# A four-part attention stack on one core: cross-attention's mask as its keys' last row, and two batches' rows normalised on ScalarE

## The chip, the core and the metric

The kernel runs on one core of a Trainium2 chip. The metric is the device time of one execution in microseconds; lower is better. Each kernel is executed several times and the median is compared. One execution is also recorded by the hardware profiler; the profile shows, for each engine of the core (TensorE as PE, its weight loads as PEld, VectorE as DVE, ScalarE as ACT, GpSimd as POOL, SyncE as SP, which issues most DMAs), what ran when.

## The reference

The reference chains four attention modules over activations of 8 batches x 256 rows x 128 columns, with a context of 8 x 64 rows x 64 columns. Modules 0 and 1 (a gated memory attention with a layer norm, and a single-head attention) run first, module 3 (an attention normalised over queries, with a layer norm) runs last. Nearly all the time goes to module 2: six layers, each of which is

```
tn = _ln(t, norm_g, norm_b)
t  = _mha(tn, tn, skv, sq, sow, sob, tgt_mask) + t      # self-attention, 16 heads of 64
tn = _ln(t, norm_g, norm_b)
t  = _mha(src, tn, ckv, cq, cow, cob, src_mask) + t     # cross-attention to the 64 context rows
tn = _ln(t, pg, pb)
t  = t + (relu(tn @ w1 + b1) @ w2 + b2)                 # feed-forward, 512 wide
```

where `_ln(x, g, b) = (x - mean) / sqrt(var + 1e-5) * g + b`, and `_mha` replaces scores at mask == 0 by -1e9 ahead of the softmax. The same norm_g and norm_b serve self-attention and cross-attention of all layers. All inputs are float32, the masks int32.

## The kernel before

**An order written out by hand.** The kernel is a plan. `at(tick, phase, fn)` files a step under a tick and a phase within it; at the end all steps are run sorted by tick and phase, and each engine is bound to execute its instructions in exactly that order. A tick is roughly one step of the attention pipeline. Nothing reorders the engines afterwards: an instruction that waits holds up everything behind it on its engine. Buffers are rotating pools: a new tile of a tag takes the place of the oldest, and waits for that one's last reader. PSUM is one pool of four tiles of two banks, for everything TensorE writes.

**A layer.** A layer takes 48 ticks: self-attention 32 (four per batch, `plan_sa`), then cross-attention 16 (two per batch, `plan_ca`), with the feed-forward (`plan_ff`) and the next layer's first self-attention projections laid over cross-attention's ticks. In the text, c is the first of the cross-attention ticks (`T_ca` in the code).

**Self-attention's ticks.** Each has two steps of scores (L939, 16 matmuls each), a VectorE pass that adds the mask and takes row minima of the negated scores (L953, eight instructions, each with a short read of its accumulator), eight exps on ScalarE (L958, each with an accumulator read), two reciprocals on VectorE (L966), eight normalising multiplications on GpSimd (L968), and 32x32 block transposes on VectorE (L978). Values (L994), the copies of the results (L299, L301), the output projection (L1012), its addition (L1019) and the next batch's projections (L902, L921) are spread over the ticks.

**Cross-attention's ticks.** The weights of queries and keys are multiplied together ahead of time, for all heads, and so are those of values and outputs. `plan_ca_weights` does that at the end of self-attention: both packed weights are transposed in blocks (L1057), written to DRAM and fetched back (L1060, L1068), regrouped by GpSimd (L1074) and multiplied on TensorE (`folded`, L1083), which gives AT (tick c-4, copied by ScalarE at L1095) and WVO (tick c-3, copied at L1093). For two batches at a time `keys_both` multiplies AT with the context (L1120, copies at L1126, into tiles of tag q); `make_values` does the same with WVO (L318, L324). Then, in each tick, `plan_weights_64` computes for 128 rows x 16 heads x 64 keys: scores (L356, 16 matmuls of 128x32 weights and 256 columns in four groups of four that run side by side), and behind each group four bfloat16 matmuls that add the mask (L363: weights that are one in the first row and zero below, times a tile `nm2` whose first row holds 0 or -1e30). ScalarE copies the scores to SBUF (L372), VectorE takes the maximum (L374), GpSimd subtracts it (L375), ScalarE takes exp (L381). One tick later VectorE sums (L385) and inverts (L386), GpSimd multiplies (L387); then VectorE transposes in blocks (L395), and a tick after that TensorE multiplies with the values (L429) and VectorE adds the result to the activations (L1145).

**Rows are normalised ahead of use.** `ahead` is called for every batch of every sublayer: mean and variance (L849, L850, L852) on VectorE, the power -0.5 (L859) on GpSimd, the normalised rows `xn` (`normal`), and the transposition on TensorE (L882) with norm_g and norm_b applied as scale and bias per partition by ScalarE (L884). `normal` is done either by ScalarE (L868, which also needs a negated mean, L855, and its product with the power, L862) or by VectorE (L873). Cross-attention and feed-forward use ScalarE, self-attention VectorE.

## Time and profile before

| | |
|---|---|
| median of 3 runs (lowest to highest) | 2411.13 us (2407.03 to 2411.5) |
| the profiled execution's own time | 2410.29 us |
| its span, first to last instruction | 2408.5 us |
| mean granted TensorE clock | 0.987 |
| TensorE busy | 2325.2 us (97%) |
| VectorE busy | 1872.3 us (78%) |
| ScalarE busy | 1707.7 us (71%) |
| GpSimd busy | 1359.1 us (56%) |
| DMA share of the instruction-issued queue q1 | 10.1% of 16 engines' span |

The six layers are nearly equal: the first scores of cross-attention (L356) of the six stand at 396.7, 765.8, 1135.0, 1502.9, 1872.2 and 2240.2 us. Matmuls overlap on TensorE and their ends are modelled, so busy time of PE is not time at its peak, and the busy time of a group of matmuls is not what it adds to the span. What an edit is worth is better read from the chain that ended last: from the last instruction back, at each step to what released it or to the instruction ahead of it on its engine. A group's line reads: line, engine, operation, written tile <- read tiles, shapes, count, busy us and mean ns of one, and the idle time ahead of it with what ended it.

### The profile page before, as it was taken

The numbers are of one execution on the slowest core, as the hardware profiler recorded it, in microseconds if no ns is written. First come the engines' busy times: TensorE is split into PE (matmuls) and PEld (weight loads), VectorE is DVE, ScalarE is ACT, GpSimd is POOL, SyncE is SP. The second block draws the span as 40 slices with busy tenths as digits, with TensorE's granted clock in tenths as the row PEclk, the third lists the DMA queues.
The fourth block names the chain that finished last, engine by engine and source line by source line (L and its number), as shares of the span: only waits on it lengthen the run. The fifth ranks groups of instructions, "written<-read, shape, count | busy, mean of one in ns | idle before, by whom it ended". The sixth has DMA issues, their size and how long they took to land.

```text
span 2408.5 us, 100346 instructions
## 1 busy us (share of the span) xinstructions
PE 2325.2 (97%) x42564; PEld 1719.9 (71%) x42564; DVE 1872.3 (78%) x6237; ACT 1707.7 (71%) x4514; POOL 1359.1 (56%) x2231
## 2 busy tenths in 40 slices
PE   7889999999999999999999999999999999999997
PEld 4557777777777777777777777777777777777775
DVE  5677887777888767888767888767888767888775
ACT  4567777667777667778667778667778667777663
POOL 2444556754556754555764555755555765455665
PEclk9989999999999999999999999999999999999998
DMA  6000022001022001012000012000013000001000
GB/s 180 2 2 20 21 73 65 2 3 30 21 64 66 11 3 30 21 56 73 12 2 26 21 45 87 12 2 18 25 40 89 21 2 18 25 26 42 2 4 16
DMA packets 102834, 76.90 MB, mean 32 GB/s; under 512 B 8113, under 2 KB 96881, under 8 KB 102386
## 3 DMA queue, kind: packets, MB, share of 16 engines
q1 hardware_dynamic: 101794, 70.16, 10.1%
q8 instruction: 335, 5.49, 0.9%
q14 instruction: 113, 0.93, 0.1%
q10 hardware_dynamic: 592, 0.33, 0.1%
HBM read 62.07 MB, written 8.39 MB: 29 GB/s over the span
## 4 chain that ended last, share of the span: by engine, by line
PE 75%; DVE 13%; ACT 5%; POOL 4%; issue 2%; DMA 0%; SPq 0%; POOLq 0%; ACTq 0%; DVEq 0%
PE sc L939 12%; PE mm L902 12%; PE mm L994 12%; PE mm L1012 6%; PE mm L921 6%; PE mm L429 6%; PE sc L356 5%; DVE e L953 3%; PE mm L1178 3%; PE mm L1161 3%; DVE eTc L978 2%; DVE m L374 2%; POOL e L968 2%; PE mm L1120 2%; PE mm L318 2%
## 5 line engine op out<-in xcount | busy, mean ns | idle before, releaser
L968 POOL TENSOR_SCALAR e<-e,rs 128x256 f32<-128x256 f32 x1536 | 702.8, 478 | 706.3 <-DVE rs L966 696.5
L958 ACT ACTIVATE e<-e,mn 128x256 f32<-128x256 f32 x1536 | 758.6, 495 | 151.3 <-DVE mn L953 146.5
L953 DVE CUSTOM_DVE_ANT_0 e<-sc,nm 128x256 f32<-128x256 f32 x1536 | 543.1, 419 | 93.4 <-PE sc L939 92.3
L978 DVE STREAM_TRANSPOSE eTc<-e 128x512 f32<-128x512 f32 x768 | 516.2, 694 | 59.4 <-POOL e L968 58.2
L939 PE MATMUL sc<-k,q 64*32 64x256 f32 x12288 | 380.8, 383 | 2.3 <-DVE o L299 1.3
L994 PE MATMUL mm<-eTc,v 32*64 32x256 f32 x12288 | 363.4, 378 | 5.7 <-ACT AT L1095 3.3
L375 POOL TENSOR_TENSOR e<-e,m 128x1024 f32<-128x1024 f32 x112 | 213.0, 1902 | 262.1 <-DVE m L374 262.1
L994 PEld LDWEIGHTS mm<-eTc,v 32*64 32x64 f32 x12288 | 277.1, 131 | 88.5 <-issue 22.2
L939 PEld LDWEIGHTS sc<-k,q 64*32 64x32 f32 x12288 | 221.8, 107 | 125.3 <-issue 51.4
L374 DVE TENSOR_REDUCE m<-e 128x16 f32<-128x1024 f32 x112 | 136.3, 1217 | 197.0 <-ACT e L372 197.0
L958 ACT ACTIVATION_READ_ACCUMULATOR e<-e,mn 128x1 f32 x1536 | 287.9, 187 | 0.0
L356 PE MATMUL sc<-q,tT 128*32 128x256 f32 x3072 | 217.0, 382 | 3.8 <-DVE t L1019 3.2
L429 PE MATMUL mm<-v,o 128*128 128x128 f32 x1536 | 197.5, 283 | 1.9 <-DVE t L1145 1.7
L429 PEld LDWEIGHTS mm<-v,o 128*128 128x128 f32 x1536 | 183.1, 195 | 19.0 <-issue 9.1
L902 PE MATMUL mm<-tT,w_sk 128*128 128x256 f32 x768 | 189.2, 389 | 0.2 <-PE mm L994 0.2
L1012 PEld LDWEIGHTS mm<-w_sow,o 128*128 128x128 f32 x1536 | 175.1, 192 | 17.6 <-issue 12.3
L921 PE MATMUL mm<-w_sv,tT 128*32 128x256 f32 x3072 | 185.6, 382 | 0.0
L1012 PE MATMUL mm<-w_sow,o 128*128 128x128 f32 x1536 | 183.6, 278 | 1.3 <-ACT WVO L1093 1.3
L387 POOL TENSOR_TENSOR e<-e,r 128x1024 f32<-128x1024 f32 x96 | 182.6, 1902 | 0.5 <-DVE r L386 0.5
L301 ACT COPY v<-mm 128x1024 f32<-128x1024 f32 x96 | 97.1, 1012 | 115.4 <-PE mm L921 115.4
L902 PE MATMUL mm<-tT,w_sq 128*128 128x256 f32 x768 | 173.6, 379 | 0.0
L902 PEld LDWEIGHTS mm<-tT,w_sk 128*128 128x128 f32 x768 | 138.3, 190 | 44.2 <-issue 29.2
(222 smaller groups left out, 3489.4 us busy)
## 6 DMA issues: line engine op xcount, KB each, us to landing
nm<-mask_d SPq DMA_DIRECT2D x192, 128.0 KB
wd<-o SPq DMA_DIRECT2D x48, 128.0 KB
w_sk<-in_L_sa_kv_dram SPq DMA_DIRECT2D x6, 512.0 KB
w_sv<-in_L_sa_kv_dram SPq DMA_DIRECT2D x24, 128.0 KB
w_sq<-in_L_sa_q_dram SPq DMA_DIRECT2D x6, 512.0 KB
w_sow<-in_L_sa_ow_dram SPq DMA_DIRECT2D x6, 512.0 KB
w_ckv<-in_L_ca_kv_dram SPq DMA_DIRECT2D x12, 256.0 KB
w_cq<-in_L_ca_q_dram SPq DMA_DIRECT2D x6, 512.0 KB
```

The costliest lines, as they stand in the source:

```text
L356: nc.tensor.matmul(sc[32 * a : 32 * a + 32, q, :], lhsT=qT()[:, qb * 32 : (qb + 1) * 32], rhs=keys()[:, a].rearrange("p h k -> p (h k)"), ...
L375: nc.gpsimd.tensor_tensor(e, e, m.unsqueeze(2).to_broadcast([P, 16, M]), ALU.subtract)
L429: nc.tensor.matmul(ps[:, :D], lhsT=eT[:, s].rearrange("p q x -> p (q x)"), rhs=vw[:, r, k, g, :], start=(s == 0), stop=(s == 7),)
L902: nc.tensor.matmul(ps[:, i * S : (i + 1) * S], lhsT=w[:, c * P : (c + 1) * P], rhs=st["tT"], start=True, stop=True,)
L921: nc.tensor.matmul(ps[32 * a : 32 * a + 32, i, :], lhsT=st["tT"][:, kb * 32 : (kb + 1) * 32], rhs=sv[:, a].rearrange("p g x -> p (g x)"), ...
L939: nc.tensor.matmul(sc[32 * a : 32 * a + 32, r, j, :], lhsT=st["q"][g][rows, a, qb * 32 : (qb + 1) * 32], rhs=st["k"][g][rows, a, :], start ...
L953: nc.vector.tensor_tensor_reduce(e[:, i, :], sc4[:, i, :], st["nm"][:, 2 * jj + i % 2, :], -1.0, 3.0 * BIG, ALU.add, ALU.min, mn[:, i : i ...
L958: nc.scalar.activation(e[:, i, :], e[:, i, :], AF.Exp, scale=-1.0, bias=mn[:, i : i + 1], accum_out=rs[:, i : i + 1],)
L968: nc.gpsimd.tensor_scalar(e[:, i, :], e[:, i, :], rs[:, i : i + 1], 1.0, ALU.mult, ALU.mult)
L978: nc.vector.transpose(eT[:, r, :, 2 * jj : 2 * jj + 2, :], e[:, 2 * r : 2 * r + 2, :].rearrange("p j (k x) -> p k j x", x=32),)
L994: nc.tensor.matmul(ops[a // 2][r * HD : (r + 1) * HD, a % 2, :S], lhsT=st["v"][kb // 4][rows, kb % 4, (2 * g + r) * HD : (2 * g + r + 1) * ...
L1012: nc.tensor.matmul(st["ps"][:, j * D : (j + 1) * D], lhsT=st["oT"][c // 4][:, c % 4, j * P : (j + 1) * P], rhs=sow[:, c, :], start=(c == 0 ...
```

## The change

**The mask.** The bfloat16 mask matmuls are gone. Instead the mask is added to the keys' last row, and that row meets a constant one on the other side. Normalised rows sum to zero over their 128 columns, so the last column is the negative sum of the others and can be left out if each of the other 127 rows of AT has the last row subtracted. For cross-attention `ahead` therefore gets `last_off` as scale (one, but zero in the last partition) and `last_on` as bias (zero, but one in the last partition) in place of norm_g and norm_b, which go into AT instead: AT is multiplied by norm_g, its last column (over the free dimension, which becomes the keys' last row) is subtracted from all, and the row sum of AT times norm_b is put into the last column. `mask_keys` then adds 0 or -1e30 to the last partition of each batch's keys, with one VectorE operation on partitions 96 to 127. `nm2` is now float32 on all 128 partitions.

**The fold.** The whole of `plan_ca_weights` starts one tick earlier; AT is made at c-5, WVO stays at c-3. The new work on AT lies between: two multiplications, a subtraction and two small copies on GpSimd, a row sum on VectorE. norm_g and norm_b are loaded once more, broadcast over partitions.

**The rows.** Self-attention's rows of batches 0 and 1 are normalised by ScalarE, the others by VectorE as before.

The core of the diff:

```diff
+    norm_rows = const.tile([P, 2, D], F32, tag="norm_rows", name="norm_rows")
+    for i, name in enumerate(("L2_norm_g", "L2_norm_b")):
+        nc.sync.dma_start(out=norm_rows[:, i, :], in_=io[name].partition_broadcast(P))
...
-    nm2 = const.tile([P, B, M], BF16, tag="nm2", name="nm2")
-    nc.vector.memset(nm2, 0.0)
-    ones0 = const.tile([P, 32], BF16, tag="ones0", name="ones0")
...
+    nm2 = const.tile([P, B, M], F32, tag="nm2", name="nm2")
+    last_on = ident[:, P - 1 : P]
+    last_off = const.tile([P, 1], F32, tag="last_off", name="last_off")
+    nc.vector.tensor_scalar(last_off, last_on, -1.0, 1.0, ALU.mult, ALU.add)
+    last_big = const.tile([P, 1], F32, tag="last_big", name="last_big")
+    nc.vector.tensor_scalar(last_big, last_on, -BIG, None, ALU.mult)
...
-                        start=True, stop=False,
-                    )
-                for a in range(4):
-                    nc.tensor.matmul(
-                        sc[32 * a : 32 * a + 32, q, :], lhsT=ones0, rhs=mask,
-                        start=False, stop=True,
+                        start=True, stop=True,
                     )
...
-        nc.vector.tensor_scalar(nm2[0:1], mi, 0.0, -BIG, ALU.is_equal, ALU.mult)
+        nc.vector.tensor_scalar(nm2, mi, 0.0, last_big, ALU.is_equal, ALU.mult)
...
-        ahead(b, (T - 6, 8.3), (T - 5, 2.6), (T - 5, 7.2), norm_g, norm_b, st, False)
+        ahead(b, (T - 6, 8.3), (T - 5, 2.6), (T - 5, 7.2), norm_g, norm_b, st, b < 2)
...
         at(T + 2, 3.6, folded("AT", 0, lambda c: st[1][:, :, c, :], HD ** -0.5))
-        at(T + 3, 3.6, folded("WVO", 1, lambda c: W["ca", l][2][:, c, :]))
+        def rows(i):
+            return norm_rows[:, i].unsqueeze(1).to_broadcast([P, HC, D])
+        def meet_bias():
+            st["z"] = big("q", shape=(P, HC, D))
+            nc.gpsimd.tensor_tensor(st["z"], st["AT"], rows(1), ALU.mult)
+        def sum_bias():
+            st["add"] = sm([P, HC], "add")
+            nc.vector.tensor_reduce(st["add"], st.pop("z"), AX.X, ALU.add)
+        def scale():
+            nc.gpsimd.tensor_tensor(st["AT"], st["AT"], rows(0), ALU.mult)
+        def lose_last():
+            last = sm([P, HC], "last")
+            nc.gpsimd.tensor_copy(last, st["AT"][:, :, D - 1])
+            nc.gpsimd.tensor_tensor(
+                st["AT"], st["AT"], last.unsqueeze(2).to_broadcast([P, HC, D]), ALU.subtract
+            )
+        def put_bias():
+            nc.gpsimd.tensor_copy(st["AT"][:, :, D - 1], st.pop("add"))
+        at(T + 2, 8.05, meet_bias)
+        at(T + 3, 2.35, scale)
+        at(T + 3, 8.05, lose_last)
+        at(T + 3, 8.7, sum_bias)
+        at(T + 4, -0.1, put_bias)
+        at(T + 4, 3.6, folded("WVO", 1, lambda c: W["ca", l][2][:, c, :]))
...
+        def mask_keys():
+            last = keys_of[b][96:].rearrange("p a c k -> p (a c) k")
+            nc.vector.tensor_tensor(
+                last, last, nm2[96:, b].unsqueeze(1).to_broadcast([32, 16, M]), ALU.add
+            )
...
-        ahead(b, (T - 4, 6), (T - 3, 2.95), (T - 2, 2.9), norm_g, norm_b, st)
+        ahead(b, (T - 4, 6), (T - 3, 2.95), (T - 2, 2.9), last_off, last_on, st)
...
+        at(T - 1, 1.9, mask_keys)
...
-        plan_ca_weights(l, T_ca - 6)
+        plan_ca_weights(l, T_ca - 7)
```

More of the change, by code (lines that the diff above doesn't have):

```diff
@@ L262, in load_mask @@
         return nm
-    nm2 = const.tile([P, B, M], BF16, tag="nm2", name="nm2")
-    nc.vector.memset(nm2, 0.0)
-    ones0 = const.tile([P, 32], BF16, tag="ones0", name="ones0")
-    nc.vector.memset(ones0, 0.0)
-    nc.vector.memset(ones0[0:1], 1.0)
+    nm2 = const.tile([P, B, M], F32, tag="nm2", name="nm2")
[4 more added lines that the diff above has]
+    nc.vector.tensor_scalar(last_big, last_on, -BIG, None, ALU.mult)
     def stats(xin, eps):
@@ L327, in values_of, with plan_weights_64 @@
         return vw
-    def plan_weights_64(tick, qt, qT, keys, values, mask, take):
+    def plan_weights_64(tick, qt, qT, keys, values, halves, take):
         tl = {}
@@ L336, in scores @@
             sc = two_banks("sc").rearrange("p (q x) -> p q x", q=4)
-            if mask is None:
+            if halves:
                 for i in range(4):
@@ L392, in turn @@
             e = tl.pop("e").rearrange("p (q h) (k x) -> p (h k) q x", q=4, x=32)
-            eT = big("k" if mask is None else "o", shape=(P, 8, 4, 32))
+            eT = big("k" if halves else "o", shape=(P, 8, 4, 32))
             for i in range(2):
@@ L436, in plan_weights_64 @@
         at(tick, 2, lower)
-        if mask is None:
+        if halves:
             at(tick + 1, 2.05, exps)
@@ L637, in mask_keys @@
         mi = big("q", dtype=I32)
-        mi = mi[0:1, : B * M].rearrange("p (b m) -> p b m", b=B)
-        nc.sync.dma_start(out=mi, in_=io["mask_Bx1xS2_if1"].rearrange("b o m -> o b m"))
-        nc.vector.tensor_scalar(nm2[0:1], mi, 0.0, -BIG, ALU.is_equal, ALU.mult)
+        mi = mi[:, : B * M].rearrange("p (b m) -> p b m", b=B)
+        nc.sync.dma_start(
+            out=mi, in_=io["mask_Bx1xS2_if1"].rearrange("b o m -> (b o) m").partition_broadcast(P)
+        )
+        nc.vector.tensor_scalar(nm2, mi, 0.0, last_big, ALU.is_equal, ALU.mult)
     mask_bf = []
@@ L773, in plan_l0 @@
             plan_weights_64(
-                T + qt, qt, lambda: st["q"], lambda: st["k"], lambda: st["VW"], None,
+                T + qt, qt, lambda: st["q"], lambda: st["k"], lambda: st["VW"], True,
                 lambda ps, qt=qt: add(qt, ps),
@@ L1130, in keys_both @@
             keys_of[b], keys_of[b + 1] = res
+        def mask_keys():
+            last = keys_of[b][96:].rearrange("p a c k -> p (a c) k")
+            nc.vector.tensor_tensor(
+                last, last, nm2[96:, b].unsqueeze(1).to_broadcast([32, 16, M]), ALU.add
+            )
         def make_values():
@@ L1149, in plan_ca @@
                 T + qt, qt, lambda: st["tT"], lambda: keys_of[b], lambda: st["VW"],
-                nm2[:, b].unsqueeze(1).to_broadcast([P, 4, M]), lambda ps, qt=qt: add(qt, ps),
+                False, lambda ps, qt=qt: add(qt, ps),
             )
```

## The prediction

> **What bounds the kernel now.** I read the page first (engine shares), then the groups by shape (the price of each operation that the change touches), then the chain that ended last, in two stretches of the second layer, and last the busy time in windows of 3.41 us. A tick of the plan is named by cross-attention's first tick, c, which starts at 765.84 us in this layer; c−4 is four ticks before it.
>
> The page's first part says that TensorE hardly rests, and the groups give the prices:
>
> ```profile
> PE 2325.2 (97%) x42564; PEld 1719.9 (71%) x42564; DVE 1872.3 (78%) x6237; ACT 1707.7 (71%) x4514; POOL 1359.1 (56%) x2231
> ```
> ```profile
> L374 DVE TENSOR_REDUCE m<-e 128x16 f32<-128x1024 f32 x112 | 136.3, 1217 | 197.0 <-ACT e L372 197.0
> ...
> L375 POOL TENSOR_TENSOR e<-e,m 128x1024 f32<-128x1024 f32 x112 | 213.0, 1902 | 262.1 <-DVE m L374 262.1
> ...
> L363 PE MATMUL sc<-nm,ones 128*32 128x256 bf16 x1536 | 112.4, 273 | 0.0
> ...
> L873 DVE TENSOR_SCALAR xn<-t,mv,rstd 128x128 f32<-128x128 f32 x96 | 50.0, 562 | 0.0
> ```
>
> The 112.4 us of L363 are not what they cost, since matmuls overlap; the chain shows that. Its pieces are start, length, engine, tile, line. First the end of self-attention, where the weights for cross-attention are folded:
>
> ```profile
> 738.79 1.11 PE sc L939 x32
> ...
> 744.14 1.85 POOL e L968 x4
> ...
> 748.54 2.64 ACT e L958 x11
> 751.19 0.77 ACT xn L868 x2
> ...
> 753.50 1.01 ACT WVO L1093
> ...
> 754.55 3.84 PE mm L1012 x32
> ```
>
> and then cross-attention:
>
> ```profile
> 787.70 1.02 ACT e L372
> ...
> 788.74 1.23 DVE m L374
> ...
> 790.04 1.92 POOL e L375
> ...
> 792.94 1.00 ACT e L372
> ...
> 800.20 1.12 DVE m L374
> ...
> 804.12 3.43 PE mm L429 x16
> ...
> 831.45 0.11 PE sc L363 x4
> ...
> 845.20 2.04 DVE xn L873 x2
> ```
>
> Seen here: a group of four mask matmuls is worth 0.11 us of chain (L363 x4), so 384 groups are 42 us, 0.44 us per tick. But TensorE does not hold the chain everywhere. Between 738.79 and 754.55 it runs through VectorE, GpSimd and ScalarE (15.8 us in which TensorE has about 13.8 us of work), and between 787.70 and 804.12 through the loop copy, maximum, subtraction, exp (787.70 to 792.94: 5.24 us a tick). TensorE reaches the end of those stretches early and waits.
>
> The windows (busy us of PE, PEld, DVE, ACT, POOL, then the granted clock):
>
> ```profile
> 801.13:804.54 3.41, 1.89 (x23) 0.99 (x12) 2.90 (x6) 2.74 (x6) 3.33 (x4) 1.00 0.00 0
> 804.54:807.95 3.41, 3.41 (x29) 2.98 (x35) 2.48 (x3) 1.79 (x3) 1.95 (x2) 0.50 0.02 5
> 1169.77:1173.18 3.41, 1.98 (x32) 0.92 (x20) 3.38 (x6) 2.22 (x5) 3.33 (x5) 1.00 0.01 2
> 1173.18:1176.59 3.41, 3.32 (x52) 2.66 (x54) 2.03 (x3) 2.44 (x5) 1.95 (x2) 1.00 0.00 0
> ```
>
> In the second layer a window with TensorE idle 1.52 us is followed by one at half clock; at the same place of the third layer 1.43 us idle is not. Four of six layers pay this at tick c+6, which then lasts 11.35 us instead of 10.11.
>
> **The change, part by part (per layer).**
>
> *The fold AT (L1083, 32 records, 1.97 us on TensorE) moves from tick c−4 to c−5.* Its DMAs and transposes (L1057, L1060, L1068) and the regrouping (L1074, 1.04 us of GpSimd) move one tick with it and keep their distances; SyncE's queue only takes two loads in another order. On TensorE it leaves a tick where the vector chain is late and enters one where the chain view shows TensorE without a break (709.09 to 738.79). The scores of c−4 start 1.97 us later, and the chain from them to L1012 starts with them: +1.97. Into it come VectorE's row sum of the bias (128x1024 to 128x8, like L374: 1.22 us) right before tick c−3's first instruction, 746.72 in this layer: +1.22. GpSimd gets three operations of 128x1024 (L375: 1.90 each). The first lies in its 2.8 us wait before 744.14. The second stands between the two normalisations of c−4 and delays one whose transpose has over a microsecond to spare; the third, with a small copy (0.2), ends at about 753.8, the power and product behind it (0.70 and 0.20) at 754.7, where ScalarE's L868 would start at 754.4 (751.19 + 1.97 + 1.22): +0.4 with the semaphores. Sum +3.6. Bounds: +1.7 if the fold itself finds slack, +4.5 if GpSimd delays the transposes too. I take 3.6.
>
> *The keys' add: VectorE, 32x1024, once per batch.* No row has it. L1019 (256 elements, 388 ns) and a 128-element addition (255 ns) give 1.04 ns per element, so 1.19 us, as L374; 1.2 taken. In c+1, c+3, c+7 VectorE waits 1.7, 3.5 and 2.5 us for ScalarE's copy just behind the place of the add, which hides it; in c+13 VectorE has room (4.4 us busy of 9.5). In c−1 it must first wait for ScalarE's key copies (759.53 to 761.58), so the eight mask instructions, the exps and ScalarE's copies behind it come about 1 us later: this eats tick c's 0.44 and no more, since ScalarE idled 0.93 there. In c+5 VectorE runs from 793.97 to 803.9 without a gap and TensorE's L429 waits at its end: the whole 1.2 is paid. In c+9 and c+11 three batches' statistics already fill VectorE, and its additions (L1145) free the PSUM tiles that the next transposes and scores take: about 1.7 us lost in all.
>
> *The mask matmuls.* Ticks c to c+2: no gain, the loop copy to exp (5.24 us a tick from 768.25 on) sets scores c+3. Ticks c+3 to c+6: one score's 0.44 at the head of the loop, minus 1.2: +0.76. Ticks c+7 to c+11: five times 0.44 = −2.2. Ticks c+12 to c+15: TensorE alone, −1.74.
>
> *Two batches' rows on ScalarE.* Batch 0's L873 pair (2.04 us on the chain) leaves the end of c+11: TensorE waits 1.17 us there, so −1.3. On ScalarE it is 0.88 us at about 841.4, where ScalarE waits 1.8 us for L1161; the extra mneg and nm (0.16, 0.20) lie in waits. From c+7 to c+11 that makes −2.2 − 1.3 + 2.0 (the 1.7 above, and 0.3 where c+8's transpose waits for L868 behind L1166) = −1.5. Batch 1 is in a stretch that TensorE sets: 0. In the first layer both lie beside cross-attention-free ticks: 0.
>
> *At the start*: two 64 KB broadcasts, a 128-row mask load and two tiny VectorE operations, far ahead of their readers: 0 (bounds −1 to +2 us in all).
>
> Sum without the clock: 3.6 + 0 + 0.76 − 1.5 − 1.74 = +1.1 us per layer, +7 us.
>
> *The clock.* Before the second fold (WVO) TensorE must wait until the masks of c−3 are read from PSUM, now about 752.8, having ended the values at about 749.7: 3.1 us idle, and some 1.4 before the values. The Trainium skill ("TensorE: Matmul & The Clock Gate", Part 1) says that the clock falls to half after a whole window of about 3.4 us idle, and warns of gaps over 3 us. By that rule no gap here, old or new, costs anything, and the sum is 2418. The rows decide: 1.5 us idle in a window of 3.41 is enough. So c−3 gets a half-clock window in every layer (1.7 us of TensorE's time, of which some 0.6 shows, the rest lies in the wait for WVO), c+6 gets it in six layers and not four (2 × 1.24 / 6 = 0.4), and c+1, where the wait before L994 grows from 0.40 to about 1.4, sometimes: 0.2. +1.2 per layer, +7 us.
>
> Total +14 us: 2410.3 (the profiled execution, 1.8 us over its span) becomes 2424; the median shown, 2411.1, becomes 2425.
>
> **The rivals.**
> - *The add hides after all.* I count 3.6 us of it per layer (0.44 + 1.2 + 1.7, and 0.3 behind it). If all is covered, each layer ends at +2.3 − 3.6 = −1.3, 2403. For: VectorE is 78% busy and waits 197 us for L372. Against: the unbroken row 793.97 to 803.9. It decides once less than 1.3 of the 3.6 shows.
> - *TensorE sets the pace throughout*: −42 for the masks, −8 for the normalisation: 2361. For: 97% busy. Against: both chain stretches above.
> - *More half clock*: two windows instead of one at c−3 and c+6 and one at c+1, up to 1.5 us more per layer: 2434.
> - *Nothing moves*: the terms cancel, 2411; the fold's 1.97 would do that with the clock unchanged.
>
> **How the numbers follow.** Forecast (2416 to 2430) 0.45; more half clock 0.18; add hidden 0.22; TensorE throughout 0.07; cancelled 0.08. A measurement of this kernel tells about 0.2% (4.8 us) from no change. Faster 0.29, same 0.08, slower 0.63. The range leaves out the fast rival and the ends: 2396 to 2438; the forecast's own is 2416 to 2430.
>
> **What would show it.** L363 gone, and scores L356 at 0.43 us per group. A gap of TensorE of some 3 us before the second L1083 in every layer, and half clock behind it. The layer's period (369.1 us) longer by 1 to 4. VectorE's chain through the add in c+5; no L873 before c+12. Wrong if the scores of c−4 find VectorE still busy (then the fold's move is free), if cross-attention's ticks c to c+6 shrink by 0.4 each, or if the period falls below 368.

## The result, and the profile after

The changed kernel takes 2413.6 us (median of 22 runs, 2412.2 to 2418.4) against 2409.9 us of the kernel before, run beside it (22 runs, 2405.4 to 2412.6). The ratio is 1.0020 with a 95% interval of 1.0013 to 1.0026: slower by 3.7 us. The forecast was slower by 14 us. The profiled execution spans 2415.3 us (before: 2408.5), 6.8 us more.

Most of the code's lines named here have moved by 1 to 6: scores of self-attention are L942 (L939 before), scores of cross-attention L362 (L356), the loop copy, maximum and subtraction L373, L375 and L376 (L372, L374, L375), the fold's matmuls L1086 (L1083), the output projection L1015 (L1012), the normalisations L871 and L876 (L868, L873). Cross-attention's later lines have moved further: the keys' copies are L1159 (L1126) and the addition of the result L1185 (L1145).

The engine shares of the page, after:

```profile
PE 2295.1 (95%) x41028; PEld 1687.7 (70%) x41028; DVE 1919.8 (79%) x6278; ACT 1715.0 (71%) x4538; POOL 1442.6 (60%) x2273
```

TensorE has 1536 instructions and 30 us of busy time less, VectorE 48 us and GpSimd 84 us more. The groups by shape, after, give the prices of what was added (columns as before: busy us, mean ns of one, idle time ahead of it):

```profile
L375 DVE TENSOR_REDUCE m<-e 128x16 f32<-128x1024 f32 x112 | 136.5, 1218 | 131.6 <-ACT e L373 130.8
...
L1167 DVE TENSOR_TENSOR q<-q,nm 32x1024 f32<-32x1024 f32 x48 | 62.1, 1293 | 4.5 <-ACT q L1159 2.6
...
L876 DVE TENSOR_SCALAR xn<-t,mv,rstd 128x128 f32<-128x128 f32 x72 | 26.5, 411 | 0.0
...
L1117 DVE TENSOR_REDUCE add<-q 128x8 f32<-128x1024 f32 x6 | 7.1, 1177 | 0.0
```
```profile
L376 POOL TENSOR_TENSOR e<-e,m 128x1024 f32<-128x1024 f32 x112 | 213.0, 1902 | 206.4 <-DVE m L375 206.4
...
L1113 POOL TENSOR_TENSOR q<-AT,norm_rows 128x1024 f32<-128x1024 f32 x6 | 14.3, 2376 | 14.8 <-ACT AT L1098 14.8
L1120 POOL TENSOR_TENSOR AT<-AT,norm_rows 128x1024 f32<-128x1024 f32 x6 | 14.2, 2367 | 0.0
L1125 POOL TENSOR_TENSOR AT<-AT,last 128x1024 f32<-128x1024 f32 x6 | 11.4, 1896 | 0.5
```

VectorE's wait ahead of the maximum fell from 197.0 us to 131.6. The keys' add (L1167) has moved in there for two thirds of it: without the add the wait is 176.1 us (experiment 2). The add takes 1.22 to 1.25 us in 38 of 48 cases, as estimated, and up to 1.65 in the rest. Two of GpSimd's three products cost 2.37 us and not the 1.90 of L376.

**Where the 6.8 us went.** The table cuts each execution into stretches, by the start in the trace of the output projection of tick c−6 and of c−2, and of the first scores of c, c+3, c+7, c+12 and c+15. A single execution's start and end vary by a few us with the clock, and the one profiled after (2417.1 us) is 3.5 us above its median, so its 6.8 us are not the 3.7 of the medians. Values are us in layers 0 to 4; the last layer, behind which no next one starts, differs from c+7 on. "Start" is from the span's start to c−6 of layer 0.

| stretch | before | after | after − before, all layers |
|---|---|---|---|
| start | 356.5 | 353.3 | −3.2 |
| c+15 to the next layer's c−6 | 219.48 | 218.75 | −3.5 |
| c−6 to c−2 (the fold) | 28.85 | 32.88 (layer 4: 33.86) | +25.2 |
| c−2 to c | 11.28 | 11.28 | −0.1 |
| c to c+3 | 19.44 | 19.50 | +0.1 |
| c+3 to c+7 | 24.19 or 25.41 | 25.03 | +0.4 |
| c+7 to c+12 | 36.86 | 35.98 | −6.0 |
| c+12 to c+15 | 27.83 | 26.52 | −6.9 |
| c+15 of the last layer to the end | 58.4 | 59.3 | +0.9 |

First the fold, in the second layer. The chain that ended last (start, length, engine, tile, line), after:

```profile
738.28 1.11 PE sc L942 x32
...
743.63 1.84 POOL e L971 x4
745.47 2.33 POOL AT L1120
747.80 1.81 POOL e L971 x4
749.62 0.15 POOL last L1124
...
749.85 1.90 POOL AT L1125
751.74 0.67 POOL rstd L862
...
752.48 0.20 POOL nm L865
...
752.71 0.88 ACT xn L871 x2
...
755.12 1.02 ACT WVO L1096
...
756.18 0.82 PE mm L1015 x5
```

Before, the chain went through GpSimd for one normalisation and was then VectorE's and ScalarE's. Now GpSimd holds it without a pause from 743.63 to 752.68: two normalisations, the scaling, the subtraction, and behind them the power (L862) and product (L865) for which ScalarE's normalised rows wait, and behind those ScalarE's copies. VectorE's sum L1117 is not on it.

Then cross-attention, the same view:

```profile
795.24 1.22 DVE m L375
...
801.50 1.22 DVE q L1167
...
802.75 1.23 DVE m L375
...
812.00 1.93 PE sc L362 x32
...
842.72 1.22 DVE q L1167
...
847.99 1.93 PE sc L362 x32
```

The add of tick c+5 is on the chain at 801.50, with VectorE busy without a gap from 795.24, and another at 842.72, in c+11. No normalisation of rows by VectorE stands ahead of the scores at 847.99. TensorE now waits for the add ahead of the scores of c+6, 2.26 us in each of the six layers; here the third (timeline: start, length, instruction, in brackets the idle time ahead of it and what ended it):

```profile
1172.83 3.02 PE L362 MATMUL sc<-q,tT 128*32 128x256 f32 x32 [2.26 <-DVE q L1167]
```

Last the clock. The busy time in windows of 3.41 us (PE, PEld, DVE, ACT, POOL, then the granted clock), after: c+6 of the second layer, c+6 of the third, and the fold of the second:

```profile
801.46:804.87 3.41, 1.94 (x32) 1.13 (x32) 3.35 (x4) 1.14 (x3) 2.90 (x5) 1.00 0.00 0
804.87:808.28 3.41, 2.39 (x17) 1.97 (x18) 2.12 (x6) 2.80 (x5) 2.94 (x2) 1.00 0.02 5
1170.10:1173.51 3.41, 1.15 (x19) 0.81 (x21) 3.24 (x10) 0.28 (x1) 3.25 (x6) 1.00 0.00 0
1173.51:1176.92 3.41, 3.41 (x29) 1.88 (x22) 3.13 (x6) 2.62 (x6) 3.05 (x3) 0.50 0.00 0
```
```profile
746.85:750.26 3.41, 0.83 (x18) 0.26 (x5) 3.41 (x18) 2.50 (x11) 3.32 (x7) 1.00 0.00 0
750.26:753.68 3.42, 3.42 (x30) 3.16 (x30) 1.75 (x5) 2.49 (x10) 3.34 (x6) 0.50 0.03 7
```

The third layer gets half clock at c+6, the second does not (TensorE is idle 2.26 us of the window ahead in one, 1.47 in the other), and c+3 to c+7 takes 25.03 us in both: VectorE, 3.1 us busy of 3.41 in the slow window, sets the end. In the fold's half-clock window GpSimd does (3.34 of 3.42, and the chain above runs through it).

### The profile page after: what moved, and what is told of

It is laid out like the page before. It is cut to its first block, busy times and chain, and to the rows that moved or that the text cites. A ratio compares the mean times of both kernels' runs of the same rounds, so it can differ in the third digit from the quotient of the medians.

```text
span 2415.3 us, 97397 instructions
## 1 busy us (share of the span) xinstructions
PE 2295.1 (95%) x41028; PEld 1687.7 (70%) x41028; DVE 1919.8 (79%) x6278; ACT 1715.0 (71%) x4538; POOL 1442.6 (60%) x2273
## 4 chain that ended last, share of the span: by engine, by line
PE 72%; DVE 13%; POOL 6%; ACT 6%; issue 2%; DMA 0%; SPq 0%; POOLq 0%; ACTq 0%; DVEq 0%
PE mm L905 14%; PE sc L942 13%; PE mm L997 12%; PE mm L924 7%; PE mm L1015 7%; PE mm L430 4%; DVE m L375 3%; PE sc L362 3%; PE mm L1218 3%; PE mm L1201 3%; POOL e L376 2%; DVE e L956 2%; ACT e L373 2%; DVE o L396 1%; POOL e L971 1%
## 5 line engine op out<-in xcount | busy, mean ns | idle before, releaser
L942 PE MATMUL sc<-k,q 64*32 64x256 f32 x12288 | 381.6, 384 | 3.2 <-ACT o L307 2.1
L376 POOL TENSOR_TENSOR e<-e,m 128x1024 f32<-128x1024 f32 x112 | 213.0, 1902 | 206.4 <-DVE m L375 206.4
L942 PEld LDWEIGHTS sc<-k,q 64*32 64x32 f32 x12288 | 222.9, 107 | 126.5 <-issue 51.9
L375 DVE TENSOR_REDUCE m<-e 128x16 f32<-128x1024 f32 x112 | 136.5, 1218 | 131.6 <-ACT e L373 130.8
L362 PE MATMUL sc<-q,tT 128*32 128x256 f32 x3072 | 189.5, 388 | 26.7 <-DVE q L1167 13.6
L1015 PEld LDWEIGHTS mm<-w_sow,o 128*128 128x128 f32 x1536 | 175.1, 192 | 19.0 <-issue 12.3
L1015 PE MATMUL mm<-w_sow,o 128*128 128x128 f32 x1536 | 184.2, 278 | 1.6 <-ACT WVO L1096 1.3
L388 POOL TENSOR_TENSOR e<-e,r 128x1024 f32<-128x1024 f32 x96 | 182.6, 1902 | 0.5 <-DVE r L387 0.5
```

What stands on the lines that cost most here:

```text
L362: nc.tensor.matmul(sc[32 * a : 32 * a + 32, q, :], lhsT=qT()[:, qb * 32 : (qb + 1) * 32], rhs=keys()[:, a].rearrange("p h k -> p (h k)"), ...
L376: nc.gpsimd.tensor_tensor(e, e, m.unsqueeze(2).to_broadcast([P, 16, M]), ALU.subtract)
L942: nc.tensor.matmul(sc[32 * a : 32 * a + 32, r, j, :], lhsT=st["q"][g][rows, a, qb * 32 : (qb + 1) * 32], rhs=st["k"][g][rows, a, :], start ...
L1015: nc.tensor.matmul(st["ps"][:, j * D : (j + 1) * D], lhsT=st["oT"][c // 4][:, c % 4, j * P : (j + 1) * P], rhs=sow[:, c, :], start=(c == 0 ...
```

## The experiments

Where an experiment's stretch is given, it is cut as in the table above.

**1. The fold one tick earlier, nothing else** (kernel before).

```diff
-        at(T + 3, 3.6, folded("WVO", 1, lambda c: W["ca", l][2][:, c, :]))
+        at(T + 4, 3.6, folded("WVO", 1, lambda c: W["ca", l][2][:, c, :]))
...
-        plan_ca_weights(l, T_ca - 6)
+        plan_ca_weights(l, T_ca - 7)
```

> The kernel before with one edit: the preparation of the folded weights starts one tick earlier, AT at c-5, WVO left at c-3. No new arithmetic. Theory of the vector chain: from the output projection of c-6 to that of c-2 a layer takes 28.85 us before; the 1.97 us of TensorE's L1083 are put ahead of the chain that decides, so 30.8 us, +12 us in all, less about 2 us if the earlier transposes relieve self-attention: 2420. Rival, TensorE's work decides: the same work in another order, 2410, and 28.9 us.

2417.1 us, ratio 1.0036 (1.0023 to 1.0049). The stretch c−6 to c−2 grew by 1.90 in every layer, to 30.75; c+15 to c−6 fell by 0.29, all of it in the four ticks ahead of c−6 (30.28 to 30.00). That the fold's transposes, which now come a tick earlier, no longer load them was not tested. The step of 1.97 holds. It leaves 32.88 − 30.75 = 2.13 us a layer for the work on AT.

**2. No add to the keys** (changed kernel, the cross-attention mask is left out).

```diff
-        at(T - 1, 1.9, mask_keys)
```

> The changed kernel without the addition of the mask to the keys: the cross-attention mask is left out. It tells what VectorE's 48 additions (1.2 us each) cost. Vector chain: c+3 to c+7 falls from 25.0 to 23.8 us, c+7 to c+12 from 36.0 to about 34, the stretch before c hardly; -3 us per layer, 2395. Rival, the addition is hidden: 2413.

2397.5 us, 0.9952 (0.9937 to 0.9966), 16 us below the changed kernel. c to c+3 fell to 19.03 (−0.47), c+7 to c+12 to 34.09 (−1.90), c+3 to c+7 to 23.77 in three layers and 25.05 in two. The two have half clock at c+6: with the add gone it shows again, at 1.28 us. All six layers have a half-clock window in the fold here, and c−6 to c−2 is 32.88 as in the layers without one.

**3. All self-attention rows on VectorE** (changed kernel).

```diff
-        ahead(b, (T - 6, 8.3), (T - 5, 2.6), (T - 5, 7.2), norm_g, norm_b, st, b < 2)
+        ahead(b, (T - 6, 8.3), (T - 5, 2.6), (T - 5, 7.2), norm_g, norm_b, st, False)
```

> The changed kernel with all self-attention rows normalised by VectorE again, as before. Forecast theory: only the end of c+11 loses, c+7 to c+12 grows from 36.0 by about 1 us, +6 us: 2420. A second theory, from the 3.2 us by which the first layer's cross-attention starts earlier: the rows of the first layer are worth 2.5 us there too, +8 us: 2422. Rival, worth nothing: 2414.

2430.5 us, 1.0086 (1.0069 to 1.0103), 17 us above the changed kernel. c+7 to c+12 grew by 2.0 to 2.2 in five layers, and c+12 to c+15 by 1.6 and 1.2 in the first two, which have a half-clock window there. The start grew by 2.2, but starts of equal code differ by as much (experiment 5). It was put at nothing in the prediction.

**4. No mask matmuls** (kernel before, the cross-attention mask is left out).

```diff
-                        start=True, stop=False,
-                    )
-                for a in range(4):
-                    nc.tensor.matmul(
-                        sc[32 * a : 32 * a + 32, q, :], lhsT=ones0, rhs=mask,
-                        start=False, stop=True,
+                        start=True, stop=True,
                     )
```

> The kernel before without the 1536 mask matmuls: the cross-attention mask is left out, nothing takes its place. It tells what the saving is worth by itself. TensorE throughout: -42 us, 2368. Vector chain: 0.44 each in c, c+3 and from c+7 on, 0 in c+1, c+2, c+4 to c+6: -4.6 us per layer, less 2.5 us for half clock in the two layers that had none at c+6: 2385.

2391.0 us, 0.9923 (0.9908 to 0.9937): 18.5 us of the 42 that 384 groups of 0.11 us make. In c+12 to c+15 and behind it TensorE alone sets the pace and all of it came (1.31 and 0.44 a layer); in c to c+3 it was 0.41, in c+7 to c+12 1.10 and not 2.2. In c+3 to c+7 it became waiting: TensorE came to the wait in c+6 earlier, was idle 1.8 to 2.0 us in a window, and all six layers got half clock there (24.8 to 25.0 in layers 0 to 4, against 24.19 for a layer without it before).

**5. Rows on ScalarE, nothing else** (kernel before).

```diff
-        ahead(b, (T - 6, 8.3), (T - 5, 2.6), (T - 5, 7.2), norm_g, norm_b, st, False)
+        ahead(b, (T - 6, 8.3), (T - 5, 2.6), (T - 5, 7.2), norm_g, norm_b, st, b < 2)
```

> The kernel before with one edit: ScalarE normalises the self-attention rows of batches 0 and 1. Theory (what the changed kernel's trace says): about 2 us at the start of layer 0 and some 2 us in each of the five boundaries between layers, at c+7 to c+12, where VectorE's 2.0 us pass was on the path (36.86 to about 35.5 there, the keys' add being absent: a little less than the 2.0 that giving the rows back to VectorE cost); five times 1.5 and 2 at the start, about 10 us: 2400. Rival one (the prediction's own sum): the pass and part of a wait in c+7 to c+11, 1.5 us a layer, nothing at the start: 2402 and the start unchanged. Rival two: the rows only paid because the keys' add loaded VectorE; without it nothing moves: 2410. The stretch from the start to layer 0's first cross-attention tells the theory from rival one, the stretch c+7 to c+12 both from rival two.

2400.2 us, 0.9969 (0.9957 to 0.998), 9 us below the kernel before. c+7 to c+12 fell from 36.86 to 35.28, and the start from 356.5 to 352.8. In the start, 2.4 us of it lie between batch 0's first projections, its first scores and its first values (13.1 + 38.1 us before, 11.4 + 37.4 here and in the changed kernel). Part of it is the clock: the kernel before has four half-clock windows in this stretch and this one three. Experiments 4 and 8, in which VectorE normalises these rows too and which also have three, take 50.3 and 50.4 us, so 1.6 us are left for the rows. The rest of the start differs by some us between executions of equal code, as its half-clock windows fall otherwise (352.95 in experiment 8, which has the start of the kernel before). The chain of the kernel before shows why, in a stretch that the prediction had not read:

```profile
103.37 1.11 DVE xn L873 x2
...
137.58 1.11 DVE xn L873 x2
```

Two pairs of rows that VectorE normalises stand on the chain of the start, 1.1 us each. The second lies in the stretch just given, the first ahead of it: from the chain's step at 94.70 us to the first projections it is 15.8 us before and 15.1 here. At the end of c+11 the chain of this experiment is TensorE's alone, where before 2.04 us of L873 stood at 845.20:

```profile
842.34 1.79 PE mm L429 x16
844.13 1.02 PE mm L318 x32
845.15 4.95 PE mm L902 x22
```

**6. The subtraction behind the power** (changed kernel).

```diff
-        at(T + 3, 8.05, lose_last)
+        at(T + 3, 8.45, lose_last)
```

> The changed kernel with one edit: the due time of the fold's subtraction of the last column (GpSimd copy and 2.33 us pass) goes from 8.05 to 8.45 in tick c-4, so that GpSimd takes the 1.84 us power of that tick, which the chain by rstd needs, before it and not behind it. Theory (GpSimd's order set the 4.03 us that the fold stretch grew by, not VectorE's sum): the stretch from the out-projection of c-6 to that of c-2 falls from 32.88 to about 31.7 to 32.1 (the 1.90 of the matmul move and what VectorE's 1.22 us sum adds stay), about 1 us a layer, 2408. If VectorE's sum is what binds, as the prediction had it, the stretch stays at 32.9 and the time at 2414. If the subtraction, now later, holds up the folded weights' second half: longer than 32.9 and slower.

2413.5 us, 1.0023 (1.0014 to 1.0032): no different from the changed kernel. c−6 to c−2 fell to between 31.87 and 32.57, but c−2 to c rose from 11.28 to between 11.34 and 12.03; the two together are 43.9 against 44.16. The chain of this kernel (third layer):

```profile
1116.01 1.10 DVE add L1117
...
1120.56 1.91 POOL AT L1125
...
1122.72 1.82 POOL e L971 x4
```

VectorE's sum is now on the chain, and the subtraction stands ahead of the next tick's normalisation, which is as tight: 0.26 us is all that the order was worth.

**7. The odd batches' add one tick earlier** (changed kernel).

```diff
-        at(T - 1, 1.9, mask_keys)
+        at(T - 1 - b % 2, 1.9, mask_keys)
```

> The changed kernel with one edit: the add of the mask to the keys' last row (1.22 us of VectorE) of the odd batches is due one tick earlier (c, c+4, ... in place of c+1, c+5, ...), so the add of batch 1's second scores is no longer right ahead of the scores of c+6. Theory (the add sits ahead of the reduction that scores(c+6) waits for): c+3 to c+7 falls from 25.03 toward the 23.8 that leaving the add out gave, and c+7 to c+12 by up to about 1; 1.5 us a layer at most, about 2405. Rival: VectorE is full over these ticks, so the add costs the same wherever it stands: c to c+3 gains about 0.5, c+3 to c+7 loses nothing, 2414.

2428.6 us, 1.0089 (1.0075 to 1.0102), slower than both expectations. c to c+3 went from 19.50 to 20.8 in the layer without half clock at c+1 and 21.1 to 21.5 in the others. In c the add is right ahead of a maximum that the loop waits for, and took 2.15 us there, while the 1.90 us product of GpSimd (L388) ran:

```profile
1166.78 2.15 DVE q L1167
...
1168.96 1.22 DVE m L375
```

c+3 to c+7 hardly got shorter: 24.8 in the layer without half clock at c+6, 25.8 to 26.1 in four with it, which is no longer hidden there. c+7 to c+12 fell by 0.9, as expected. All 17 adds of over 1.8 us in this trace overlap that product of GpSimd, and of the other 31 (at most 1.45 us) none does; no run takes the product away from beside the add and leaves the rest. So the place of the add matters, but the given one is the better of the two.

**8. TensorE kept busy in c+6** (kernel before).

```diff
-    def ahead(b, stats_at, normal_at, tT_at, g, bias, st, on_scalar=True):
+    def ahead(b, stats_at, normal_at, tT_at, g, bias, st, on_scalar=True, warm=0):
...
             ps = tp_tile()
+            for _ in range(warm):
+                nc.tensor.transpose(ps[:, S : S + P], ident, ident)
...
-        ahead(b, *steps, pre_g[:, l : l + 1], pre_b[:, l : l + 1], st)
+        ahead(b, *steps, pre_g[:, l : l + 1], pre_b[:, l : l + 1], st, True,
+              9 if b == 0 else 0)
```

> The kernel before with nine extra 128x128 transposes of the identity, whose result nobody reads, in the transposition of batch 0's feed-forward input, in the TensorE gap ahead of the scores of c+6, where four layers fall to half clock. Theory (the half clock there costs 1.22 us a time, and idle time inside one 3.41 us window brings it on): the granted clock shows no half there, c+3 to c+7 is 24.2 in all of layers 0 to 4 (25.4 before in three or four), 4 to 5 us in all: 2405. Rival (the wait ahead of the scores is VectorE's, and the half clock is covered by it as in the changed kernel): the stretch stays, 2410; slower by up to 0.5 us a layer if the extra transposes are late themselves.

2405.3 us, 0.9985 (0.9977 to 0.9994), 3.8 us below. In the kernel before, TensorE waits in c+6 behind the scores and ahead of a transposition, for rows that ScalarE normalises:

```profile
802.91 0.94 PE L882 MATMUL tp<-ident,xn 128*128 128x128 f32 x4 [1.20 <-ACT xn L868]
```

The nine transposes stand right ahead of this one. In their run 0.4 us of TensorE's idle time is left where 1.52 were, and the clock stays whole:

```profile
797.00:800.40 3.40, 3.00 (x27) 2.16 (x20) 2.56 (x5) 3.06 (x6) 3.40 (x3) 1.00 0.00 0
800.40:803.80 3.40, 3.40 (x64) 2.75 (x64) 2.78 (x4) 2.44 (x4) 1.94 (x2) 1.00 0.02 5
```

c+3 to c+7 is 24.20 in all of layers 0 to 4. So it is the idle time that brings the half clock on, and in the kernel before it costs 1.2 us each time.

**9. The query fold in the middle of self-attention** (changed kernel; both weights are turned and fetched eight ticks earlier, the regrouping is split in two halves, the value fold stays).

```diff
-            at(T - 6 + i, 8.7, lambda i=i: turned(i))
-            at(T - 4 + i, -0.5, lambda i=i: fetched(i))
-        at(T + 1, 8.05, regrouped)
-        at(T + 2, 3.6, folded("AT", 0, lambda c: st[1][:, :, c, :], HD ** -0.5))
+            at(T - 14 + i, 8.7, lambda i=i: turned(i))
+            at(T - 12 + i, -0.5, lambda i=i: fetched(i))
+        at(T + 1 - 8, 8.05, lambda: regrouped(0))
+        at(T + 1, 8.05, lambda: regrouped(1))
+        at(T + 2 - 8, 3.6, folded("AT", 0, lambda c: st[1][:, :, c, :], HD ** -0.5))
...
-        at(T + 2, 8.05, meet_bias)
-        at(T + 3, 2.35, scale)
-        at(T + 3, 8.05, lose_last)
-        at(T + 3, 8.7, sum_bias)
-        at(T + 4, -0.1, put_bias)
+        at(T + 2 - 8, 8.05, meet_bias)
+        at(T + 3 - 8, 2.35, scale)
+        at(T + 3 - 8, 8.05, lose_last)
+        at(T + 3 - 8, 8.7, sum_bias)
+        at(T + 4 - 8, -0.1, put_bias)
```

> The changed kernel with the fold of the query weights (its transfer, matmuls, and the GpSimd and VectorE work on AT) eight ticks earlier, c-13 to c-11, in the middle of self-attention, where TensorE was busy all the time and GpSimd half of it; the value fold stays at c-3. Theory (at c-5 to c-3 it is GpSimd's 7.1 us a layer ahead of the powers that made 2.1 of the 4.03 us; TensorE's time for the matmuls, 1.9, is paid anywhere in self-attention): the stretch from c-6 to c-2 falls from 32.88 to about 28.9, the one from c+15 to c-6 rises from 218.75 to about 220.7, 2.1 us a layer less: 2401. Rival (GpSimd's powers are just as tight in the middle): both sums stay, 2414.

2406.4 us, 0.9991 (0.9983 to 0.9999), 7 us below the changed kernel. The projection that the stretches are cut at lies elsewhere here, so c+15 to c−2 is compared: 251.63 after, 250.53 here, 249.94 with the fold moved alone (experiment 1, which still has 0.44 of mask matmuls in c+15). 1.1 of the 2.1 expected us came back. Where the other microsecond stays was not found.

**10. TensorE kept busy in c+6** (changed kernel, the edit of experiment 8).

> The changed kernel with the same nine extra transposes ahead of the scores of c+6 that took the half clock away in the kernel before. Theory (in the changed kernel VectorE's add makes TensorE wait there anyway, so half clock ahead of it costs nothing): c+3 to c+7 stays at 25.03 in every layer, 2414. Rival (the prediction's clock term: each half clock there costs 1.2 us): about three windows less, 2410. If the transposes were in the way themselves: up to 0.9 us a layer slower, 2419.

2417.2 us, 1.0034 (1.0021 to 1.0046). The transposes did not keep the clock up: c+6 of layers 0, 2 and 4 got half clock as in the changed kernel, the transposes themselves then ran at half speed, and c+3 to c+7 took 25.77 there; in layers 1 and 3, with a whole clock, 25.03. They were in the wrong place. In the changed kernel the long wait is ahead of the scores, for VectorE's add, and the transposes stand behind them (third layer):

```profile
1173.80 3.23 PE L362 MATMUL sc<-q,tT 128*32 128x256 f32 x32 [2.26 <-DVE q L1169]
1176.95 1.54 PE L884 MATMUL tp<-ident 128*128 128x128 f32 x9
```

So this run does not tell what the half clock costs; that layers with it and without it take the same 25.03 in the changed kernel does.

**11. The mask put into the keys' last row by TensorE** (changed kernel).

```diff
+                for r in range(2):
+                    nc.tensor.matmul(
+                        ps[:, r], lhsT=sel,
+                        rhs=nm2[:, b : b + 2].rearrange("p b m -> p (b m)")
+                        .unsqueeze(1).to_broadcast([P, 4, 2 * M]),
+                        start=True, stop=False,
+                    )
...
-                            start=True, stop=True,
+                            start=False, stop=a == 3,
...
-        at(T - 1, 1.9, mask_keys)
```

(`nm2` is again bfloat16 with the mask in its first row; `sel` is zero but for a one in row 0, column 127.)

> The changed kernel with the mask put into the keys' last row by TensorE and not by VectorE: four bf16 matmuls of 512 columns for each two batches, summed in PSUM with the keys' own product, and no add. Theory (the add's 1.22 us on VectorE is what the ticks c to c+12 pay for): the stretches of the run without the add, c to c+3 19.0, c+3 to c+7 23.8, c+7 to c+12 34.1, and between nothing and all of TensorE's time, worked out from 0.11 us for a bf16 mask matmul of 256 columns in the kernel before: 16 a layer of 0.22, 3.5 us. 2398 with all of it hidden, 2418 with none; likeliest a third of it, 2405. Rival (the gain of the run without the add came from the mask left out, which changes the data): c to c+12 as with the add.

2420.1 us, 1.0048 (1.0034 to 1.0062). Hardly any of the matmuls' time was hidden, where a third on the path had been held likeliest:

```profile
L1151 PE MATMUL mm<-nm,sel 128*128 128x512 bf16 x96 | 29.0, 384 | 0.0
```

That is 4.8 us a layer of busy time, and most of it showed: c−2 to c 12.45 (11.28), c to c+3 19.56 (19.03 without the add), c+3 to c+7 24.73 or 26.3 with half clock (23.77), c+7 to c+12 34.81 (34.09). Summed without half clock, that is about 3.4 us a layer of TensorE, the 3.5 that the expectation had with none hidden, against about 3.6 for the add (0.47, 1.26 and 1.90 in experiment 2, each without half clock).

**12. Both: experiments 9 and 11 in one.**

> Both edits in one: the fold in the middle of self-attention and the mask put in by TensorE. If their gains lie in different stretches they add up: the time of the run with the mask in PSUM less the gain of the run with the fold moved, about 2392, and so below the kernel before. Rival: the ticks between share a limit and less than the sum is seen, 2400 or more.

2408.9 us, 1.0000 (0.9992 to 1.0008). The fold's gain adds (11 us below experiment 11), but the sum is no better than the kernel before.

**13. Rows on ScalarE and TensorE kept busy in c+6** (kernel before, the edits of experiments 5 and 8).

> The kernel before with two edits: ScalarE normalises the self-attention rows of batches 0 and 1, and the nine transposes ahead of the scores of c+6. Apart from each other they gave 9 and 4 us. Theory: the first acts at the start and in c+7 to c+12, the second in c+3 to c+7, so they add: 2396, with c+3 to c+7 at 24.2 and c+7 to c+12 at 35.3 in layers 0 to 4. Rival: with the rows gone from VectorE the windows fall otherwise and the half clock comes back elsewhere: 2400.

2397.1 us, 0.9947 (0.9935 to 0.996): the fastest complete kernel of the study, 12 us below the kernel before. c+3 to c+7 is 24.18 and c+7 to c+12 35.28 in layers 0 to 4: the two edits add.

**14. The fold without its bias part** (changed kernel; the norm's bias is missing from the scores).

```diff
-        at(T + 2, 8.05, meet_bias)
...
-        at(T + 3, 8.7, sum_bias)
-        at(T + 4, -0.1, put_bias)
```

> The changed kernel with the fold's bias part left out (GpSimd's first product of 2.38 us, VectorE's sum, the write back of it); the scaling and the subtraction stay. The norm's bias is then missing from the scores. Theory (GpSimd's subtraction ahead of the power decides, and VectorE's sum is 0.3 us behind it): 32.88 falls to about 31.5 to 32.6 in c-6 to c-2, 2406 to 2412. If the subtraction alone decides, 32.9; if the bias is all of the 2.1 us, 30.8 and 2401.

2418.5 us, 1.0037 (1.0026 to 1.0048), though it has less to do. c−6 to c−2 stayed at 32.88. c−2 to c stayed at 11.28 in two layers and took 12.6 to 12.9 in four, which have a half-clock window there:

```profile
753.39:756.80 3.41, 1.77 (x36) 1.01 (x37) 2.68 (x9) 3.34 (x6) 3.41 (x8) 1.00 0.38 114
756.80:760.21 3.41, 3.41 (x18) 3.41 (x17) 3.34 (x17) 3.41 (x15) 1.07 (x4) 0.50 0.00 0
```

In the changed kernel TensorE waits 1.60 us ahead of the value fold and 0.98 in it (second layer). Here the first is 0.48, and there is a wait ahead of the next scores instead:

```profile
754.56 1.10 PE L942 MATMUL sc<-k,q 64*32 64x256 f32 x32 [2.09 <-ACT o L307]
```

So its half clock fell behind c−2, where TensorE sets the pace: 1.3 to 1.6 us each.

**15. VectorE's sum cut short** (changed kernel; the sum takes 8 of 128 elements and is not written back, so the bias is missing from the scores).

```diff
+        def free_z():
+            st["add"] = sm([P, HC], "add")
+            nc.vector.tensor_reduce(st["add"], st.pop("z")[:, :, :8], AX.X, ALU.add)
...
-        at(T + 3, 8.7, sum_bias)
-        at(T + 4, -0.1, put_bias)
+        at(T + 3, 8.7, free_z)
```

> The changed kernel with VectorE's sum cut to the first 8 of 128 elements and not written back; GpSimd's three products stay. The scores lack the norm's bias. The prediction's step (VectorE's 1.22 us sum is on the path): 32.88 falls by 1.2 to 31.7, 2406. Theory of the chain (GpSimd's subtraction holds the power): 32.9 or at most 0.3 less, 2412 to 2414.

2420.9 us, 1.0048 (1.0035 to 1.0062). c−6 to c−2 is 32.88 to 32.90; c−2 to c is 11.28 in the two layers without half clock there and 12.3 to 12.9 in four. In the given order the sum is worth nothing.

**16. The fold without scaling and subtraction** (changed kernel; the keys keep their mean and are not multiplied by the norm's scale).

```diff
-        at(T + 3, 2.35, scale)
-        at(T + 3, 8.05, lose_last)
```

> The changed kernel with the scaling and the subtraction left out (4.5 us of GpSimd a layer); bias product, VectorE's sum and write back stay. The keys are then not scaled by the norm and keep their mean. Theory of the chain: 32.88 falls to where VectorE's sum decides, 31.7 to 32.6, as with the subtraction behind the power; if GpSimd is all of the 2.1 us, 30.8 and 2401; by the prediction's step (0.4 of GpSimd) 32.5.

2410.3 us, 1.0004 (0.9996 to 1.0012). c−6 to c−2 fell to 31.87 in four layers, 1.01 less (to 32.54 and 32.26 in the first two, which was not followed up). Now VectorE's sum is on the chain (second layer):

```profile
741.88 1.10 DVE add L1117
742.98 0.33 DVE e L956
...
745.88 3.25 PE mm L1086 x30
```

31.87 − 1.10 is 30.77, the 30.75 of the fold's move alone. So beyond the move there are two ways through the fold: by VectorE's sum, which makes it 1.1 us longer, and by GpSimd's scaling and subtraction, which make it 2.1 us longer (experiment 14, where they are left and the rest is gone). The longer counts, and shortening the other gains nothing.

## Why the prediction was right in its sign and wrong in its size

By the steps, in us per layer unless said otherwise:

- *The fold moved, +1.97.* Right: 1.90. What it gives back ahead of c−6 (0.29, experiment 1) was not seen.
- *The bias sum on VectorE, +1.22, and GpSimd, +0.4.* Right in kind, mis-sized. The prediction had GpSimd's way end 0.4 us behind VectorE's and went by the later one, so the two terms together, 1.6, are GpSimd's. It measured 2.13: VectorE's sum is off the chain (experiment 15; by itself it makes 1.1, experiment 16), and GpSimd runs without a pause through the scaling and the subtraction, up to the power for which the rows wait. The scaling cost 2.37 us and not 1.90, which is most of the difference.
- *The keys' add.* 1.19 predicted, 1.22 measured. In c−1 it ate tick c's 0.44 (c to c+3 is 19.50 against 19.44), in c+5 it is paid in full (801.50), and c+3 to c+7 is 25.03 − 24.19 = +0.84 without the clock, against +0.76. In c+7 to c+12 it is worth 1.90 (experiment 2), against 1.7 and 0.3. All right.
- *The mask in c+7 to c+11, −2.2.* Mis-sized: 1.10 (experiment 4). The rows there: −1.3 predicted, −1.58 (experiment 5). With the add that makes −1.10 − 1.58 + 1.90 = −0.8; the stretch has −0.88, the prediction −1.5. The 0.11 us of a group were worth that only where TensorE sets the pace.
- *c+12 to c+15, −1.74.* Right: −1.31 for three ticks and −0.44 for c+15's scores, which the table has in the next stretch. The last layer has less (−0.38 for its three ticks).
- *The start, 0 with bounds of −1 and +2.* The step that failed second: "in the first layer both lie beside cross-attention-free ticks: 0". They lie on the chain of the start (103.37 and 137.58), and moving them to ScalarE gained some 2 to 3 us (experiment 5).
- *The clock, +7 us in all.* The step that failed first. Without the clock, the stretches sum up to 6 × 4.03 + 6 × 0.84 − 6.0 − 6.9 − 3.6 = +12.7 us, the last being 5 × 0.73 for c+15 to c−6; the prediction had 7, too little by 2.6 in the fold and 3.0 in c+7 to c+11. So the work was put too low and the clock too high; that the two errors in part cancelled in the +14 is luck. With start, end and clock it is 6.8. The half clock itself went the other way: four layers had paid for it at c+6 before (three times 1.22 in the table, 1.02 in the last layer), 4.7 us. After, c−3 and c+6 do get half-clock windows, as foreseen (in four layers and in three), but there VectorE, with the add in its chain (c+6), and GpSimd with its products (c−3) end later than the slowed TensorE, so its slowness lies inside a wait. Layers with and without it take the same 25.03 and 32.88. Only layer 4, with two windows in a row, paid 0.98 (as layer 1 of experiment 11 did, with two as well). In the profiled execution the clock's term is −4.7 + 1.0 = −3.7 us and not +7.

The prediction had put 0.6 of c−3's 1.7 us and all of c+6's on the path; it asked how often the half clock would come and not what else would be late at that moment. It was right to go by the row and not by the rule of the Trainium skill ("TensorE: Matmul & The Clock Gate", Part 1), which asks for a whole idle window: experiments 4 and 14 and the third layer above show half clock behind windows in which TensorE was idle 1.6 to 2.3 us of 3.41, and experiment 8 none once most of the idle time was filled. That the sum by the rule, 2418, was nearer to 2413.6 than the forecast of 2425 is due to these waits, which hid the half clock, not to the rule.

Of the rivals, "the add hides" fell (experiment 2: 16 us), "TensorE throughout" too (experiment 4: 18.5 of 42). "More half clock" came true in part in number (eight windows from the fold to c+15 of the six layers where there were four, but none at c+1 and two in a row only once), not in cost. "Nothing moves" (2411) came nearest in number, and terms did cancel, but not as it had it, by the fold's 1.97 alone with the clock unchanged.

The whole change is three parts that were worth: rows on ScalarE −9 (experiment 5); mask matmuls out −18.5 (4) and the add +16 (2); the fold's move and its new work +24 (from the table; no run has them alone). They need not add up, as they meet in the same stretches and through the clock; they do add to about +12.5, and 3.7 was measured. How much of the difference is the clock was not taken apart.

## What to carry to other kernels

A lower clock costs only where the slowed engine ends last: before counting half-clock windows, ask for each which engine's work the next step is waiting for. Where work is added to two engines that run side by side, the longer addition counts, not the sum, and a removal may do nothing but move an engine's wait, and its slow window, to a place where it is on the path (experiments 4, 14 and 15 took work away and gained less than nothing or half of it). Idle work that is to keep the clock up has to stand ahead of the instruction that waits (experiment 8); behind it, it only adds to the time (experiment 10). Take the parts of a change one by one: here a single expression, the rows of two batches on ScalarE, with nine idle transposes, made 2397.1 us, while the change as a whole made 2413.6.

## What the runs showed of the hardware that was not expected

- Half clock came behind windows of 3.41 us with far less than the whole window idle, but not by one bound. From the first fold to the last c+15 of all eighteen traces, no window behind one at whole clock with under 1.52 us of idle TensorE has half clock (some 10 000 windows), all 70 behind one with more than 1.91 have it, and between the two 22 of 84 (1.52 in the kernel before and 1.64 in experiment 14 with it, 1.58 and 1.78 in experiment 15 without). At the end of the program it came behind 0.97 (at 2391.74 us in the kernel before). The ends of matmuls are modelled in the trace, which may be part of the spread.
- Equal layers get different clocks: with a layer period of 369.96 us (108.4 windows) the same idle time falls into one window in layers 0, 2 and 4 and over two in layers 1 and 3, as the windows don't follow the program: in the changed kernel half-clock windows start at 750.26, 1173.52 and 1490.96 us, which is 124.0 and 93.0 windows apart.
- GpSimd's product of 128x1024 with a row that is broadcast over the middle dimension took 2.35 to 2.40 us in all runs that have it, that with a value broadcast over the last dimension 1.90.
- A bfloat16 matmul of 512 columns by 128x128 weights took 0.30 us of busy time each (29.0 us for 96), and some seven tenths of that showed on the path (3.4 of 4.8 us a layer).
